# Values computed once a token and dealt to overlapping key blocks through DRAM, in a fused four-part kernel with a planned order

## The chip, the cores and the metric

One core of a Trainium2 chip runs the whole kernel. The engines named here are PE (matmuls; PEld is its weight load), DVE (vector), ACT (activations), POOL (general purpose) and SP, which only issues DMAs. The metric is device time in microseconds, the median of several runs; lower is better.

## The reference

Input `x` is (16, 256, 128) in fp32. Four parts follow each other, each normalised: a linear attention, a mixture of experts, a linear attention with feature maps, and then a stack of six layers of windowed attention and a gated feed-forward. Only this last stack, called the layer stage below, is touched by the change. One of its attention layers, with 16 heads of 64 and windows of 32 tokens:

```
qkv = x @ Wqkv
q, k, v = (sh(q), sh(k), sh(v))
q = l2norm(q) * qs
k = l2norm(k) * ksc
q = q * cos * scale + rotate_half(q) * sin * scale
k = k * cos * inv + rotate_half(k) * sin * inv
...
bk2, bv2 = (look(bk), look(bv))
mask = (it < jb) | (it > jb + w) | (jb == -1)
sim = jnp.einsum('bhwie,bhwje->bhwij', bq, bk2) * QK_SCALE
sim = jnp.where(mask, -jnp.finfo(sim.dtype).max, sim)
attn = jax.nn.softmax(sim, -1)
out = jnp.einsum('bhwij,bhwje->bhwie', attn, bv2)
...
return out @ Wo
```

`look` puts the window before in front of each window, so that a window of 32 queries sees 64 keys and each key and value is used by two windows. Each layer adds its result to x, then a layernorm, two products with an exact Gelu gate and a third product are added as well.

## The kernel before

Tokens lie in tiles of 128 (four windows). A sequence has two tiles (`TPS`), a unit two sequences (`SPU`), and there are eight units; the layer stage therefore does 6 x 32 = 192 tiles. x stays in SBUF, transposed (`xs`, features on the partitions), with 32 columns of zeros ahead of each sequence for the window before the first.

The stages before the layers are written in order. The layer stage is not: every piece of work is a `step` with an engine, an estimated duration in us, the steps that it follows, the buffers that it takes and uses, and a rank (the running number of its tile, lower first). `Plan.run` plays this through once at build time, with its own estimates, a lag after each step (`LAG`) and a price for changing the activation table (`SWITCH`), and issues each step when its turn comes. The result is a fixed order of instructions on each engine; on the chip every engine goes through its own list in that order and waits where an operand is missing. Buffers are counted: PSUM is four `pair`s of two banks (a `bank` is half of one).

A tile in `projections` (lines 738 to 834): `product` makes q, then k, in a pair each (L748); ACT squares them (L801); DVE multiplies with the cosine and sine tables (L755, L762) and sums the squares (L771); POOL adds the two products (L810). `norms` calls `inv_norm`, eleven small DVE operations on 128x32 values (L726 to L735), three Newton rounds from a guess by bits. POOL scales q and k by it (L777), PE transposes them (L783) and ACT copies them into `qT` and `kT` (L789).

A tile in `attention` (lines 836 to 977): `scores` is 64 small matmuls, 64x32 by 64 columns (L851). In fp32 a matmul is issued as two instructions, with a weight load for each, so this is 128 matmul records and 128 weight loads. DVE adds the mask in PSUM (`mask`, L860), takes the maximum (`top`, L864) and subtracts it on the way to SBUF (`below`, L869); ACT takes exp (L878); PE transposes (L899), ACT copies (L956). `values` computes v anew for every key block: each of the four blocks of 64 tokens is the stationary operand, twice, for the even and the odd heads (L885), and ACT copies the result to `va` (L892). `mix` multiplies the exponentials with `va`, which has a column of ones so that the sum comes with it (L911); DVE divides (L922, L923), PE transposes, ACT copies to `oT` (L929).

`output` runs once a sequence: 8 matmuls over 256 columns (L985), then DVE adds to x (L994). `feed_forward` runs once a unit; its Gelu needs another activation table than exp, and is preceded by a table load. `Seq.gate` lets the projections of a tile start only when `below` of the tile three before (`AHEAD`) is done. The weights of a layer are loaded by `fetch_a` and `fetch_f` on SP into one of two sets of buffers, for the layer after the next use.

Of the kernel before, what the change touches and what calls it, by code (L numbers as in the profile page):

```python
# [10 lines left out]
F32 = mybir.dt.float32  # L11
# [6 lines left out]
P = 128  # L18
# [15 lines left out]
AHEAD = 3  # L34
NEXP = 8
# [14 lines left out]
class Step:  # L50


    def __init__(self, eng, work, fn, after, takes, uses, rank, table):
        self.eng, self.work, self.fn, self.rank = eng, work, fn, rank
        self.takes, self.uses, self.table = takes, uses, table
        self.next, self.wait = [], 0
        for b in (*takes, *uses):
            b.left += 1
        for s in after:
            s.next.append(self)  # L60
            self.wait += 1


class Plan:
# [3 lines left out]
    LAG = 0.12  # L68
    SWITCH = 1.3

# [4 lines left out]
    def step(self, eng, work, fn, after=(), takes=(), uses=(), rank=0, table=None):  # L75
        s = Step(eng, work, fn, [a for a in after if a is not None], takes, uses, rank, table)
        self.steps.append(s)
        return s
# [30 lines left out]
    def run(self):  # L109
# [11 lines left out]
        now, table, opened = 0.0, None, {}  # L121
        left = len(self.steps)
        self.log = []
        while left:
            moved = True
            while moved:
                moved = False
                for eng, heap in ready.items():
# [3 lines left out]
                    while heap and len(back) < 64:  # L132
                        item = heapq.heappop(heap)
                        s = item[2]
                        if s.table and opened and s.table not in opened:
                            back.append(item)
                            continue
                        kinds = [b.kind for b in s.takes]
                        if all(self._fits(kinds, k) for k in set(kinds)):
                            got = s  # L140
                            break
                        back.append(item)
# [27 lines left out]
                    heapq.heappush(events, (now + work + self.LAG, count, got))  # L170
# [16 lines left out]
        self.end = now  # L187

# [18 lines left out]
def tile_kernel(ctx: ExitStack, tc: tile.TileContext, a: dict, out: bass.AP):  # L207
# [64 lines left out]
    def load_attn_weights(wp, i):  # L272
        w = {}
        w["qkv"] = load(wp, [P, 3 * INNER], a["L1_ffn_Wqkv"][i], "d_wqkv")
        w["o"] = load(
            wp, [P, 8, P], a["L1_ffn_Wo"][i].rearrange("(c p) d -> p c d", p=P), "d_wo"
        )
        w["sc"] = load_bc(wp, 4 * DH, a["qk_scale"][i], "d_sc")
        return w

    def load_ffn_weights(wp, i):
# [395 lines left out]
    with ExitStack() as st:  # L677
# [3 lines left out]
        sd = st.enter_context(tc.tile_pool(name="sd", bufs=4))  # L681
# [6 lines left out]
        for b in range(NB):  # L688
# [9 lines left out]
            "va": several(cd, 2, [P, NB, 8, DH + 1], "d_va"),  # L698
# [6 lines left out]
            "oT": several(cd, 2, [P, 8, SEQ], "d_oT"),  # L705
# [6 lines left out]
        for va in slots["va"]:  # L712
            pool.memset(va[:, :, :, DH : DH + 1], 1.0)
# [9 lines left out]

        def inv_norm(x, n):

            dve.tensor_scalar(x, x, 1e-24, None, ALU.max)  # L726
            y = sd.tile([P, n], F32, name="d_ny")
            t = sd.tile([P, n], F32, name="d_nt")
            dve.tensor_scalar(
                y.bitcast(I32), x.bitcast(I32), -0.5, 1597463007.0, ALU.mult, ALU.add  # L730
            )
            for _ in range(3):
                dve.tensor_tensor(t, y, y, ALU.mult)
                dve.scalar_tensor_tensor(t, t, -0.5, x, ALU.mult, ALU.mult)
                dve.scalar_tensor_tensor(y, t, 1.5, y, ALU.add, ALU.mult)  # L735
            return y

        def projections(q, t):
# [34 lines left out]
            def norms():  # L773
                o.rn = inv_norm(o.ss.rearrange("p g h -> p (g h)"), 2 * HEADS)
# [18 lines left out]
            for qk in range(2):  # L793
                pj, sq, t1, t2 = Buf("pair"), Buf("sq"), Buf("t1"), Buf("t2")
                mm = step(
                    "pe", 1.72, partial(product, qk, pj), [*q.ready, *q.loaded, q.gate(t)],
                    [pj], rank=rank,
                )
                s = step(
# [5 lines left out]
                a2 = step("dve", 1.14, partial(second, qk, pj, t2), [mm, q.tabbed], [t2], [pj], rank)  # L805
                reds.append(step("dve", 1.14, partial(squares, qk, sq), [s, *reds], [], [sq], rank))
# [8 lines left out]
            nm = step("dve", 2.5, norms, reds, rank=rank)  # L815
# [4 lines left out]
            for qk in range(2):  # L820
# [3 lines left out]
                tn = step("pe", 0.88, partial(turn, t1s[qk], pz), [m], [pz], [t1s[qk]], rank)  # L824
# [11 lines left out]
        def attention(q, t):  # L836
# [4 lines left out]
            pS, e, va, eT, y = Buf("pair"), Buf("e"), Buf("va"), Buf("eT"), Buf("y")  # L841

            def scores():

                for c in range(8):
# [12 lines left out]
            def mask():  # L858
                s3 = pS.t.rearrange("p (h k) -> p h k", k=2 * WIN)
                dve.tensor_tensor(s3, s3, bc(win[:, t, :], [P, HEADS, 2 * WIN], 1), ALU.add)  # L860

            def top():
                o.m = sd.tile([P, HEADS], F32, name="d_m")
                dve.tensor_reduce(  # L864
                    o.m, pS.t.rearrange("p (h k) -> p h k", k=2 * WIN), AX.X, ALU.max
                )

            def below():
                dve.tensor_tensor(  # L869
                    e.t.rearrange("p c a k -> p a c k"),  # L870
                    pS.t.rearrange("p (a c k) -> p a c k", a=2, k=2 * WIN),
                    bc(o.m.rearrange("p (a c) -> p a c", a=2), [P, 2, 8, 2 * WIN], 3),
                    ALU.subtract,
                )
# [5 lines left out]
            def values(b2, pv):  # L880
                wv = q.w["qkv"][:, 2 * INNER :].rearrange("p (c a d) -> p a c d", a=2, d=DH)
                for j in range(2):
                    x0 = t * P + (2 * b2 + j) * WIN
                    for par in range(2):
                        pe.matmul(  # L885
                            pv.t[par * DH : (par + 1) * DH, j * 512 : (j + 1) * 512],
                            lhsT=q.x[:, x0 : x0 + 2 * WIN], rhs=wv[:, par, :, :],
                            start=True, stop=True,
                        )

            def put_values(b2, pv):
                act.copy(  # L892
                    va.t[:, 2 * b2 : 2 * b2 + 2, :, 0:DH],
                    pv.t.rearrange("p (j c d) -> p j c d", j=2, d=DH),
                )

# [7 lines left out]
            def mix(hh, po):  # L904
                for k in range(4):
                    c = 4 * hh + k
                    for par in range(2):
                        r = slice(par * DH, (par + 1) * DH)
                        s0 = par * 512 + k * (DH + 1)
                        for b in range(NB):  # L910
# [3 lines left out]
                                rhs=va.t[r, b, c, :], start=True, stop=True,  # L914
# [13 lines left out]
            def put_out(pz):  # L928
                act.copy(  # L929
                    q.oT.t[:, :, t * P : (t + 1) * P],  # L930
                    pz.t.rearrange("p (c n) -> p c n", n=P),
                )

            sc = step("pe", 1.9, scores, [o.done[0], *q.turned[: t + 1]], [pS], [qT, kT], rank)
            mk = step("dve", 1.15, mask, [sc], [], [pS], rank)
            tp = step("dve", 1.15, top, [mk], [], [pS], rank)
            be = step("dve", 1.15, below, [tp], [e], [pS], rank)
            ex = step("act", 0.98, exps, [be], [], [e], rank, ("exp", 0))
            q.soft.append(be)
            vs = []  # L940
            for b2 in range(NB // 2):
                pv = Buf("pair")
                v = step(
                    "pe", 1.94, partial(values, b2, pv), [*q.ready, *q.loaded, mk], [pv], [], rank
                )
                vs.append(
                    step(
                        "act", 0.97, partial(put_values, b2, pv), [v],
                        [] if b2 else [va], [pv] + ([va] if b2 else []), rank,
                    )  # L950
                )
            pz = Buf("pair")
            te = step("pe", 0.88, partial(turn, e, pz), [ex], [pz], [e], rank)
# [5 lines left out]
            for hh in range(2):  # L959
                po = Buf("pair")  # L960
                mx = step("pe", 0.75, partial(mix, hh, po), [pe_, *vs], [po], [eT, va], rank)
                ds.append(
                    step(
                        "dve", 0.85, partial(divide, hh, po), [mx],
# [4 lines left out]
            ty = step("pe", 0.88, partial(turn, y, py), ds, [py], [y], rank)  # L969
            if t == 0:  # L970
                q.oT = Buf("oT")
            q.outs.append(
                step(
                    "act", 0.97, partial(put_out, py), [ty],
                    [] if t else [q.oT], [py] + ([q.oT] if t else []), rank,
                )
            )

        def output(q):

            pr = Buf("bank")

            def product():
                for c in range(8):
                    pe.matmul(  # L985
                        pr.t[:, :SEQ], lhsT=q.w["o"][:, c, :], rhs=q.oT.t[:, c, :],
                        start=(c == 0), stop=(c == 7),
                    )

            def add():  # L990
                for h2 in range(2):
                    hp = slice(h2 * DH, (h2 + 1) * DH)
                    xo = q.x[hp, WIN + h2 : WIN + h2 + SEQ]
                    dve.tensor_tensor(xo, pr.t[hp, :SEQ], xo, ALU.add)  # L994

            rank = q.rank + 1
# [269 lines left out]
```

## Time and profile before

Three runs took 5848.07, 5855.04 and 5859.02 us. The profiled execution took 5849.97 us.

| | |
|---|---|
| span of the profiled execution | 5848.2 us |
| instructions | 153345 |
| granted PE clock, mean | 0.942 of full speed |
| DMA packets, volume | 29195, 40.16 MB |
| first projection (L748) to last feed-forward sum (L1073) | 1647.3 to about 5814 us |

The profile shows one execution. Busy times are unions of an engine's instructions of a group; "idle before" is the time in which the engine stood just before instructions of a group, with what ended that wait. PE's instructions overlap each other, so a group's busy time over its number is the better price of one than the mean duration. A wait for several things is put down to the one that came last. The rows of digits cut the span into 40 equal slices of 146 us, each digit being tenths.

The mean of one and the number, for the groups in the layer stage that the diff touches and that are not shown below:

| group | number | mean us |
|---|---|---|
| scores L851, PE (busy 309.2 us in all) | 24576 | 0.232 |
| mix L911, PE (busy 301.1 us in all) | 24576 | 0.228 |
| mask L860, DVE | 192 | 1.228 |
| top L864, DVE | 192 | 1.220 |
| below L869, DVE | 192 | 1.218 |
| norm, L733, L734, L735, DVE | 576 each | 0.192 |
| output sum L994, DVE | 192 | 0.423 |
| exp L878, ACT | 192 | 1.059 |
| copy to oT L929, ACT | 192 | 1.010 |

### The profile page before, as it was taken

Reading aid. Unit: us, or ns where it says so; the run is one execution under the profiler, and the core shown is the slowest. Engines: PE = TensorE matmul, PEld = TensorE weight load, DVE = VectorE, ACT = ScalarE, POOL = GpSimd, SP = SyncE. Lnnn points to the kernel's source line nnn. Section 1 sums busy time; section 2 is a strip of 40 time slices with the busy share of each in tenths; the row PEclk is TensorE's granted clock in tenths of the full one; section 3 lists DMA queues with packets and bytes.
Section 4 is the critical chain, followed back from the end, with each engine's and each line's share of the span. In section 5 each row is a group of like instructions: output and inputs, shape, how many; then the busy total and the mean of one; then the engine's idle time right before and its main releaser. Section 6 shows DMA issues by size and latency. Waiting matters only on the chain. (4 is left out here: it accounts for less than half of the span.)

```text
span 5848.2 us, 153345 instructions
## 1 busy us (share of the span) xinstructions
PE 4866.8 (83%) x69216; PEld 3086.3 (53%) x69216; DVE 4182.3 (72%) x7764; ACT 2325.8 (40%) x2701; POOL 1951.1 (33%) x964
## 2 busy tenths in 40 slices
PE   4677778787788888888888888898898888888886
PEld 3444566566655555555555555555555555555554
DVE  3333777777777777777678777777777777777775
ACT  1343112111134444444444444444444444444443
POOL 0000222222234344344344334334334434434432
PEclk7898899999999999999999999999999999999998
DMA  1000000000000000000000000000000000000001
GB/s 37 13 1 20 1 2 2 4 3 2 2 25 2 2 2 13 10 2 2 2 17 6 2 2 2 21 2 2 2 2 21 2 2 2 2 2 2 2 2 30
DMA packets 29195, 40.16 MB, mean 7 GB/s; under 512 B 5118, under 2 KB 24060, under 8 KB 27772
## 3 DMA queue, kind: packets, MB, share of 16 engines
q1 hardware_dynamic: 28540, 30.35, 1.7%
q8 instruction: 543, 8.90, 0.6%
q14 instruction: 112, 0.92, 0.1%
HBM read 26.15 MB, written 4.19 MB: 5 GB/s over the span
## 5 line engine op out<-in xcount | busy, mean ns | idle before, releaser
L810 POOL TENSOR_TENSOR d_t<-d_t,d_t 128x1024 f32<-128x1024 f32 x384 | 905.3, 2363 | 1717.1 <-DVE d_t L762 1242.4
L777 POOL TENSOR_TENSOR d_t<-d_t,d_ny 128x1024 f32<-128x1024 f32 x384 | 722.7, 1903 | 520.4 <-DVE d_ny L735 515.9
L748 PE MATMUL pp<-d_wqkv,xs 128*128 128x512 f32 x1536 | 776.4, 636 | 85.0 <-ACT d_oT L929 49.6
L885 PE MATMUL pp<-d_wqkv,xs 128*64 128x512 f32 x3072 | 753.5, 624 | 76.2 <-DVE d_t L762 75.2
L755 DVE TENSOR_TENSOR d_t<-pp,d_tab 128x1024 f32<-128x1024 f32 x384 | 467.8, 1218 | 392.7 <-PE pp L748 392.6
L801 ACT ACTIVATE d_sq<-pp 128x1024 f32<-128x1024 f32 x384 | 388.6, 1025 | 756.2 <-PE pp L748 250.6
L892 ACT COPY d_va<-pp 128x1024 f32<-128x1024 f32 x384 | 383.5, 1011 | 530.5 <-PE pp L885 529.5
L783 PE MATMUL pp<-ident,d_t 128*128 128x128 f32 x3072 | 414.0, 282 | 119.5 <-ACT d_qT L789 85.3
L762 DVE TENSOR_TENSOR d_t<-pp,d_tab 128x1024 f32<-128x1024 f32 x384 | 467.1, 1216 | 50.3 <-ACT d_sq L801 50.3
L783 PEld LDWEIGHTS pp<-ident,d_t 128*128 128x128 f32 x3072 | 354.3, 145 | 246.3 <-issue 158.9
L569 POOL TENSOR_TENSOR c_e<-c_e,c_sm 128x2048 f32<-128x2048 f32 x64 | 231.7, 3621 | 757.0 <-DVE c_sm L568 682.1
L748 PEld LDWEIGHTS pp<-d_wqkv,xs 128*128 128x128 f32 x1536 | 279.4, 200 | 375.5 <-issue 228.9
L771 DVE TENSOR_REDUCE d_ss<-d_sq 128x16 f32<-128x1024 f32 x384 | 464.9, 1211 | 1.4
L885 PEld LDWEIGHTS pp<-d_wqkv,xs 128*64 128x64 f32 x3072 | 202.2, 142 | 489.1 <-issue 344.1
L851 PE MATMUL pp<-d_kT,d_qT 64*32 64x64 f32 x24576 | 309.2, 232 | 157.2 <-issue 103.8
L851 PEld LDWEIGHTS pp<-d_kT,d_qT 64*32 64x32 f32 x24576 | 266.1, 108 | 225.0 <-issue 158.9
L911 PE MATMUL pp<-d_va,d_eT 64*32 64x65 f32 x24576 | 301.1, 228 | 85.5 <-issue 41.5
L985 PE MATMUL pp<-d_oT,d_wo 128*128 128x256 f32 x1536 | 357.1, 385 | 1.8 <-ACT d_oT L929 1.3
L911 PEld LDWEIGHTS pp<-d_va,d_eT 64*32 64x32 f32 x24576 | 261.1, 106 | 180.6 <-issue 90.7
L564 ACT ACTIVATE c_e<-c_e 128x2048 f32<-128x2048 f32 x64 | 122.4, 1912 | 566.2 <-DVE c_e L562 552.3
L985 PEld LDWEIGHTS pp<-d_oT,d_wo 128*128 128x128 f32 x1536 | 284.0, 190 | 113.0 <-ACT f_h L1051 38.5
L929 ACT COPY d_oT<-pp 128x1024 f32<-128x1024 f32 x192 | 193.9, 1010 | 331.7 <-PE pp L899 252.3
(172 smaller groups left out, 8440.2 us busy)
## 6 DMA issues: line engine op xcount, KB each, us to landing
d_wqkv<-L_ffn_Wqkv SPq DMA_DIRECT2D x6, 1536.0 KB, 7.1
d_wo<-L_ffn_Wo SPq DMA_DIRECT2D x6, 512.0 KB, 4.0
xin<-L_attn_x SPq DMA_DIRECT2D x8, 256.0 KB, 2.9
keep<-xu SPq DMA_DIRECT2D x8, 256.0 KB, 2.0
d_y<-keep SPq DMA_DIRECT2D x8, 256.0 KB, 2.7
out<-d_y SPq DMA_DIRECT2D x8, 256.0 KB, 2.3
d_w<-L_ffn_W SPq DMA_DIRECT2D x6, 341.0 KB, 3.0
b_w<-b_w SPq DMA_DIRECT2D x3, 576.0 KB, 7.4
```

The costliest lines, as they stand in the source:

```text
L748: pe.matmul(pj.t[:, hf * 512 : (hf + 1) * 512], lhsT=xj, rhs=q.w["qkv"][:, c : c + 512], start=True, stop=True,)
L755: dve.tensor_tensor(t1.t, heads(pj.t), bc(q.lay.tab[:, 0, t, cc], hs, 1), ALU.mult)
L762: dve.tensor_tensor(t2.t.rearrange("p h (x d) -> p h x d", x=2), swapped(pj.t), bc(q.lay.tab[:, 1, t, cc].rearrange("p (x d) -> p x d", x= ...
L771: dve.tensor_reduce(o.ss[:, qk, :], sq.t, AX.X, ALU.add)
L777: pool.tensor_tensor(t1.t, t1.t, bc(o.rn[:, qk * HEADS : (qk + 1) * HEADS], hs, 2), ALU.mult)
L783: pe.transpose(pz.t[:, c * P : (c + 1) * P], t1.t[:, 2 * c : 2 * c + 2, :].rearrange("p h d -> p (h d)"), ident,)
L801: lambda sq=sq, pj=pj: act.activation(sq.t, heads(pj.t), AF.Square),
L810: lambda t1=t1, t2=t2: pool.tensor_tensor(t1.t, t1.t, t2.t, ALU.add),
L851: pe.matmul(pS.t[b * WIN : (b + 1) * WIN, s0 : s0 + 2 * WIN], lhsT=qT.t[r, c, b * WIN : (b + 1) * WIN], rhs=kT.t[r, c, k0 : k0 + 2 * WIN], ...
L885: pe.matmul(pv.t[par * DH : (par + 1) * DH, j * 512 : (j + 1) * 512], lhsT=q.x[:, x0 : x0 + 2 * WIN], rhs=wv[:, par, :, :], start=True, st ...
L911: pe.matmul(po.t[b * WIN : (b + 1) * WIN, s0 : s0 + DH + 1], lhsT=eT.t[r, c, b * WIN : (b + 1) * WIN], rhs=va.t[r, b, c, :], start=True, s ...
L985: pe.matmul(pr.t[:, :SEQ], lhsT=q.w["o"][:, c, :], rhs=q.oT.t[:, c, :], start=(c == 0), stop=(c == 7),)
```

## The change

The planner gets a lag for each engine instead of one for all, 2 us for a DMA, and a rule: a step of more than 32 PE instructions is put off while, with it, more than 256 PE instructions would be issued within 3.6 us. `scores` is cut into four steps and `mix` into two for each half.

The mask is added on the way from PSUM to `e` in SBUF, `top` reads `e`, and `below` runs on POOL, in place. The norm's guess comes from ACT, as exp(-0.5 ln x), with one Newton round on DVE.

`values` multiplies a tile of 128 tokens once with the weights of v. ACT copies the result to `vs`, which has the columns of ones; SP writes it to a DRAM buffer `dv` of the sequence (`away`), 32 rows of zeros standing ahead of it, and reads it back into `va` (`windows`) with the overlapping rows, for the even heads to the lower 64 partitions and for the odd heads to the upper ones. The output product and its addition to x run for each tile; the addition waits for all steps of the sequence that read x. q, k, v weights keep two places and the other weights of a layer have one, loaded after their last use in the layer before.

```diff
-    LAG = 0.12
+    LAG = {"pe": 0.25, "act": 0.15, "dve": 0.12, "pool": 0.15, "sp": 2.0}
     SWITCH = 1.3
+
+    BLOCK, SPAN = 256, 3.6
...
+                        if s.count > 32 and self._dense(s, now, past, events):
+                            back.append(item)
+                            continue
...
+    def _dense(self, s, now, past, events):
+
+        room = self.BLOCK - s.count
+        for t, c in reversed(past):
+            room -= c
+            if room < 0:
+                wait = t + self.SPAN - s.work
+                if wait > now + 1e-6:
+                    self.unique -= 1
+                    heapq.heappush(events, (wait, self.unique, None))
+                    return True
+                return False
+        return False
...
-            "va": several(cd, 2, [P, NB, 8, DH + 1], "d_va"),
+            "va": several(cd, 3, [P, NB, VR], "d_va"),
+            "vs": several(cd, 2, [P, 2, VR], "d_vs"),
+            "dv": several(dr, 2, [WIN + SEQ, 2, VR], "d_dv"),
...
-            "oT": several(cd, 2, [P, 8, SEQ], "d_oT"),
+            "oT": several(cd, 3, [P, 8, P], "d_oT"),
...
-            def norms():
-                o.rn = inv_norm(o.ss.rearrange("p g h -> p (g h)"), 2 * HEADS)
+            def floor():
+                o.ss = o.ss.rearrange("p g h -> p (g h)")
+                dve.tensor_scalar(o.ss, o.ss, 1e-24, None, ALU.max)
+
+            def guess():
+                o.rn = sd.tile([P, 2 * HEADS], F32, name="d_rn")
+                act.activation(o.rn, o.ss, AF.Ln)
+                act.activation(o.rn, o.rn, AF.Exp, scale=-0.5)
+
+            def refine():
+                r = sd.tile([P, 2 * HEADS], F32, name="d_rt")
+                dve.tensor_tensor(r, o.rn, o.rn, ALU.mult)
+                dve.scalar_tensor_tensor(r, r, -0.5, o.ss, ALU.mult, ALU.mult)
+                dve.scalar_tensor_tensor(o.rn, r, 1.5, o.rn, ALU.add, ALU.mult)
...
-            nm = step("dve", 2.5, norms, reds, rank=rank)
+            fl = step("dve", 0.22, floor, reds, rank=rank)
+            gu = step("act", 0.45, guess, [fl], rank=rank, table=("exp", 0))
+            nm = step("dve", 0.68, refine, [gu], rank=rank)
...
             def mask():
-                s3 = pS.t.rearrange("p (h k) -> p h k", k=2 * WIN)
-                dve.tensor_tensor(s3, s3, bc(win[:, t, :], [P, HEADS, 2 * WIN], 1), ALU.add)
+                dve.tensor_tensor(
+                    e.t.rearrange("p c a k -> p a c k"),
+                    pS.t.rearrange("p (a c k) -> p a c k", a=2, k=2 * WIN),
+                    win[:, t, :].unsqueeze(1).unsqueeze(1).to_broadcast([P, 2, 8, 2 * WIN]),
+                    ALU.add,
+                )
...
             def below():
...
+                e3 = e.t.rearrange("p c a k -> p (c a) k")
+                pool.tensor_tensor(e3, e3, bc(o.m, [P, HEADS, 2 * WIN], 2), ALU.subtract)
...
+            def values():
+                xj = q.x[:, WIN + t * P : WIN + (t + 1) * P]
+                for hf in range(2):
+                    c = 2 * INNER + hf * 512
+                    pe.matmul(
+                        pv.t[:, hf * 512 : (hf + 1) * 512], lhsT=xj,
+                        rhs=q.w["qkv"][:, c : c + 512], start=True, stop=True,
+                    )
+
+            def put_values():
                 act.copy(
-                    va.t[:, 2 * b2 : 2 * b2 + 2, :, 0:DH],
-                    pv.t.rearrange("p (j c d) -> p j c d", j=2, d=DH),
-                )
+                    vs.t.rearrange("p a (c d) -> p c a d", d=DH + 1)[:, :, :, 0:DH],
+                    pv.t.rearrange("p (c a d) -> p c a d", a=2, d=DH),
+                )
+
+            def away():
+                sp.dma_start(out=q.dv.t[WIN + t * P : WIN + (t + 1) * P], in_=vs.t)
+
+            def windows():
+
+                row = 2 * VR
+                for par in range(2):
+                    src = q.dv.t[t * P : t * P + 2 * WIN, par, :]
+                    sp.dma_start(
+                        out=va.t[par * 2 * WIN : (par + 1) * 2 * WIN],
+                        in_=bass.AP(
+                            tensor=src.tensor, offset=src.offset,
+                            ap=[[row, 2 * WIN], [WIN * row, NB], [1, VR]],
+                        ),
+                    )
...
+            for g in range(4):
+                sc.append(
+                    step(
+                        "pe", 0.48, partial(scores, g), [o.done[0], *q.turned[: t + 1], *sc[-1:]],
+                        [] if g else [pS], [qT, kT] + ([pS] if g else []), rank, count=64,
+                    )
+                )
+            mk = step("dve", 1.15, mask, sc, [e], [pS], rank)
+            tp = step("dve", 1.14, top, [mk], [], [e], rank)
+            be = step("pool", 1.95, below, [tp], [], [e], rank)
...
+            vm = step("pe", 1.76, values, [*q.ready, *q.loaded, sc[-1]], [pv], [], rank, count=8)
+            ve = step("act", 0.97, put_values, [vm], [vs], [pv], rank)
+            vw = step(
+                "sp", 0.1, away, [ve], [] if t else [q.dv], [vs] + ([q.dv] if t else []), rank
+            )
+            q.dealt.append(vw)
+            vd = step("sp", 0.2, windows, q.dealt, [va], [q.dv], rank)
...
+                            "pe", 0.38, partial(mix, hh, g, po), [pe_, vd, *mx], [] if g else [po],
+                            [eT, va] + ([po] if g else []), rank, count=64,
...
+            mo = step("pe", 1.8, product, [os_, *q.loaded_o], [pr], [oT], rank, count=32)
+            q.sums.append((add, mo, pr, rank))
...
+            ls = step("sp", 0.3, fetch_sc, last.get(("t", i - 1), []), rank=base)
+            la = step("sp", 6.0, fetch_qkv, last.get(("qkv", i - 2), []), rank=base)
+            lo = step("sp", 3.0, fetch_o, last.get(("o", i - 1), []), rank=base)
+            lf = step("sp", 3.0, fetch_f, last.get(("f", i - 1), []), rank=base)
...
+                    for add, mo, pr, rank in q.sums:
+                        adds.append(step("dve", 0.6, add, [mo, *q.read], [], [pr], rank))
```

## The prediction

> **What bounds the kernel now.** I read the page's rows of busy time first, then the same engines over the six layers alone, then what PE waited for there, then the groups of instructions.
>
> ```profile
> PE 4866.8 (83%) x69216; PEld 3086.3 (53%) x69216; DVE 4182.3 (72%) x7764; ACT 2325.8 (40%) x2701; POOL 1951.1 (33%) x964
> PE   4677778787788888888888888898898888888886
> DVE  3333777777777777777678777777777777777775
> PEclk7898899999999999999999999999999999999998
> ```
>
> From the twelfth slice on, nothing changes any more: that is the layer stage, the only part that the change touches. It runs from the first projection (1647.3 us) to the last feed-forward sum (5814 us). The answer for this stretch, with length, then busy time of PE, weight load, DVE, ACT, POOL, then the granted clock:
>
> ```profile
> 1647.30:5814.00 4166.70, 3626.28 (x62696) 2193.10 (x62696) 3127.83 (x5676) 1929.15 (x2021) 1672.81 (x816) 0.96 0.02 6
> ```
>
> 4166.7 us for 6 x 16 x 2 = 192 tiles are 21.70 us a tile. PE is busy 18.89 of them (87%), DVE 16.29 (75%), ACT 10.05, POOL 8.71. So PE bounds the stage, with 540 us idle. Its largest waits there (us in total, times, longest):
>
> ```profile
> PE pp L851 <- issue: 103.8, 61, 2.6
> PE pp L783 <- ACT d_qT L789: 85.3, 46, 2.1
> PE pp L885 <- DVE d_t L762: 75.2, 59, 2.4
> PE pp L851 <- ACT d_kT L789: 51.8, 47, 1.1
> PE pp L748 <- ACT d_oT L929: 49.6, 45, 1.1
> PE pp L911 <- issue: 41.5, 37, 2.5
> ```
>
> Two kinds: "issue", where no operand is missing (151 us with its small rows), and evacuations that come late (230 us by ACT, 133 by DVE). The first kind in the order of time, at a scores burst followed by a mix:
>
> ```profile
> 3026.35 1.15 PEld L911 LDWEIGHTS pp<-d_va,d_eT 64*32 64x32 f32 x106
> 3026.36 1.29 PE L911 MATMUL pp<-d_va,d_eT 64*32 64x65 f32 x104
> 3029.89 0.66 PE L911 MATMUL pp<-d_va,d_eT 64*32 64x65 f32 x23 [2.24 <-issue]
> 3030.48 3.78 PE L748 MATMUL pp<-d_wqkv,xs 128*128 128x512 f32 x4
> ```
>
> After some 230 small instructions PE stands 2.24 us although nothing holds it; the following projection takes 3.78 us for what is 1.88 elsewhere. Scores and mix are 256 PE instructions each (128 matmuls and their weight loads), run in 1.5 us, so I read this as the instruction stream arriving too slowly.
>
> **The parts.** The groups that I price with (busy, mean ns):
>
> ```profile
> L777 POOL TENSOR_TENSOR d_t<-d_t,d_ny 128x1024 f32<-128x1024 f32 x384 | 722.7, 1903 | 520.4 <-DVE d_ny L735 515.9
> L748 PE MATMUL pp<-d_wqkv,xs 128*128 128x512 f32 x1536 | 776.4, 636 | 85.0 <-ACT d_oT L929 49.6
> L885 PE MATMUL pp<-d_wqkv,xs 128*64 128x512 f32 x3072 | 753.5, 624 | 76.2 <-DVE d_t L762 75.2
> L892 ACT COPY d_va<-pp 128x1024 f32<-128x1024 f32 x384 | 383.5, 1011 | 530.5 <-PE pp L885 529.5
> L985 PE MATMUL pp<-d_oT,d_wo 128*128 128x256 f32 x1536 | 357.1, 385 | 1.8 <-ACT d_oT L929 1.3
> L1051 ACT ACT_TABLE_LOAD x48 | 61.6, 1283 | 0.9
> ```
>
> *Values once a token.* Today 16 instructions a tile cost 753.5 us over the stage; afterwards four of the projection's own shape, half of the 1536 at L748, so 388 us. PE: **-365 us**, as PE is the bound. One of the two copies at L892 goes (-192 us of ACT, not on the path).
>
> *Output product per tile.* 32 instructions of 128 columns replace 16 of 256 in a sequence. Stage C has this very shape (L639): 512 instructions, 65.2 us, 0.127 us each, so 3072 x 0.127 = 391 against 357. **+34 us**. Its evacuation is only cut differently. The addition to x becomes 384 x 2 halves of 128 columns instead of 192 of 256; by the 0.29 us of the 128-column addition at L643 that is 384 x 0.29 = 111 against 81 us of DVE, +30. It waits now for every reader of x in its sequence; PE has issued them long before.
>
> *Scores in four steps, mixes in two, with a limit of 256 PE instructions in 3.6 us.* The work is the same; what can go is the issue wait, 0 to -151 us. A tile has about 650 PE instructions, 9.1 us at that rate, in some 20 us, so there is room. I take two thirds, **-100**.
>
> *DVE gets lighter.* `below` leaves (192 x 1.218 = 234 us); of the norm's eleven small operations four stay, so L729 (some 35 us) and two thirds of 3 x 110.6 go, 256 us. With the +30 DVE falls from 3128 to about 2670 us, 64%. The scores' pair of banks comes free after the mask, two DVE operations earlier than now. Of the 133 us in which PE waits for DVE I take **-50** (0 to -133). The new lags in the planner (0.25 us behind PE, where 0.12 stood) may also remove ACT waits; I count nothing for them.
>
> *`below` on POOL.* Its row is L777, also with a broadcast operand: 1.903 us, +365 us on POOL, 2038 in all, half of the stage. It queues there behind the two scalings (3.77 us in a row) and the two additions (2.36 each), with exp behind it, and the projections three tiles on wait for it. In between stands a margin of two tiles: **+20** (0 to +130, the 0.69 us excess each time).
>
> *Ln and Exp in the norm.* Two activations of 128x32; the nearest row, the sigmoid at L433 with this shape, took 0.198 us. The planner counts 0.45 for both, with no switch of tables.[...] If the sets are chosen function by function, each tile pays two loads: by the row 1.283 each, 2.57 us a tile, 493 us on ACT.[...] I give two loads 85%. ACT then goes to 1929 - 192 + 493 + 77 = 2307 us, 55%: not the bound. But behind the loads in ACT's queue stand squares, exponentials and evacuations, one for every 2 us of PE work; and the refinement, the two POOL scalings and the transposes of q and k come 2.5 us later than planned. ACT idles almost half the time, so it has caught up after some 5 us, with two evacuations late, which I price at 1 us of PE a tile: **+190** (0 if the joint set is chosen or the delay is hidden; +493 if all stands on PE).
>
> *The way through DRAM.* 128 rows of 4160 bytes out (532 KB), then two transfers of 532 KB each back. Neighbours (KB each, us to landing):
>
> ```profile
> d_wqkv<-L_ffn_Wqkv SPq DMA_DIRECT2D x6, 1536.0 KB, 7.1
> d_wo<-L_ffn_Wo SPq DMA_DIRECT2D x6, 512.0 KB, 4.0
> ```
>
> and 341 KB in 3.0. So 3.3 us out and 5.3 back (1065 KB, between the 4.0 and the 7.1), with three issues of about 0.35: 9.6 us, where the planner counts 0.1 + 2 + 0.2 + 2 = 4.3. From the scores' end: values 1.9, copy 1.0, way 9.6, so 12.5 us. Beside it runs the softmax, which in one undisturbed tile of the trace took 10.7 us from the end of the scores (4022.1) to the mix (4032.84), and which gets longer by the POOL queue and ACT's loads. The two ends nearly tie; mix is first in rank, so the planner sets it where it believes the rows have landed, and PE then waits with everything behind it. I take half a microsecond a tile, **+90** (0 to 192 x 5.1 = +980).
>
> *Instructions and data on the same engines.* 543 instruction packets carry 8.9 MB; 307 MB now join them, some 5 to 9 us of every tile. A fetch that meets them comes late: **+20** (0 to +150).
>
> *Weights and set-up.* The output and feed-forward weights have one place instead of two, so each layer loads them after the last use in the layer before. The first new use lies a tile (about 20 us) or more behind, the landing takes 4.0: hidden; uncovered 5 x 4 = 20. The scales and zeroed rows at the start: **+5**.
>
> Sum: -365 + 34 - 100 - 50 + 20 + 190 + 90 + 20 + 5 = **-156 us**, so 5850 (the profiled execution: span 5848.2 and 1.8 around it) becomes 5694. The median of the runs is 5855, 0.1% above it; I say **5695**.
>
> **Rivals.**
>
> *All is hidden* (15%): the joint set, or ACT's slack absorbs the loads; DMAs inside the softmax's time. -365 + 34 - 120 - 70 + 60 + 10 = -451, **5400**. For it: PE and DVE, the two fullest engines, both lose over 9%. Against: the order on each engine is fixed by a plan that is wrong by microseconds on two links.
>
> *The way through DRAM ends last* (26%), slower: at the first mix of each tile PE waits for the windows. Without the DMA's term the sum is -246 us, so from 1.3 us a tile on it decides. At half of the 5.1, 2.55 us x 192 = 490: 5850 - 246 + 490 = **6095**. For it: the planned 4.3 us against rows that give over 9. Against: other tiles' PE work can already lie between, and the softmax is as long.
>
> *The table loads stand wholly on PE* (14%): 493 instead of 190, **5998**.
>
> The forecast's own case, 5500 to 5838, has 40%; 5% are left for no change, within 0.2%, which is about what this measurement can tell. So faster 55%, same 5%, slower 40%. The range, 5430 to 6090, leaves out the lower half of the first rival and the upper half of the second.[...]
>
> **What will show it.** Values at half of the projection's busy time; no rows of PE waiting for "issue" at scores and mix; ACT_TABLE_LOAD near 430 in the layers (two a tile and those around Gelu), or about 95 if the joint set serves; PE's waits at mix named by the DMA, at transposes and projections by ACT; DVE near 2670 us; landings of 3 to 6 us. I am wrong if the windows take much more than 5.3 us, if the loads cost PE nothing or everything, or if the limit on instructions leaves PE standing for want of other steps.

## The result, and the profile after

The changed kernel takes 6158 us (6146 to 6162, four runs) where the kernel before takes 5852: a ratio of 1.052, 95% interval 1.050 to 1.053. It was forecast to be faster. The profiled execution took 6159.61 us, with a span of 6157.8.

The page's row of busy time, then the layer stage alone (1650.7 us, the first projection, to 6124.4, the last feed-forward sum; length, busy time of PE, weight load, DVE, ACT, POOL, granted clock, share of the DMA engines, GB/s):

```profile
PE 4811.9 (78%) x68448; PEld 3222.4 (52%) x68448; DVE 3878.6 (63%) x6420; ACT 2703.8 (44%) x3256; POOL 2313.6 (38%) x1157
```

```profile
1650.70:6124.40 4473.70, 3568.45 (x61928) 2326.60 (x61928) 2824.66 (x4334) 2309.03 (x2578) 2036.19 (x1013) 0.90 0.30 74
```

The stage grew from 4167 to 4474 us, by 307; that is the whole difference but for 3 us of set-up. Two things are to be seen. PE is idle for 905 us instead of 540. And PE is busy for 3568 us, only 58 less than before, although 365 us of matmuls left; the granted clock (the share of full speed at which PE was let run) fell from 0.96 to 0.90. What PE waited for in the layers (us in total, times, longest):

```profile
PE pp L958 <- DMA d_va<-d_dv: 393.6, 226, 5.9
PE pp L807 <- POOL d_t L801: 53.5, 30, 6.6
PE pp L946 <- ACT d_e L911: 51.4, 25, 4.6
PE pp L958 <- ACT d_eT L1017: 39.1, 25, 2.3
```

L958 is the mix: it waits for the windows of values, 2.05 us a tile. By kind, all rows of this view come to 394 us for the DMA (0 before), 220 for ACT (234), 220 for DVE (142), 54 for POOL (12) and 12 for issue (151). The transfers (KB each, median us to landing) and the table loads:

```profile
d_va<-d_dv SPq DMA_DIRECT2D x384, 520.0 KB, 6.7
d_dv<-d_vs SPq DMA_DIRECT2D x192, 520.0 KB, 3.2
```

```profile
L791 ACT ACT_TABLE_LOAD x192 | 246.3, 1283 | 3.4
L792 ACT ACT_TABLE_LOAD x192 | 246.3, 1283 | 3.4
```

One tile in the order of time, from its values to its mix (start us, us, engine, line):

```profile
3004.62 1.88 PE L917 MATMUL pp<-d_wqkv,xs 128*128 128x512 f32 x4
...
3006.36 1.28 ACT L792 ACT_TABLE_LOAD   x1
...
3007.79 1.00 ACT L923 COPY d_vs<-pp 128x1024 f32<-128x1024 f32 x1
...
3008.82 0.33 SPq L929 DMA_DIRECT2D d_dv<-d_vs  x1
...
3011.56 1.24 SPq L936 DMA_DIRECT2D d_va<-d_dv  x2
...
3014.42 1.01 ACT L1017 COPY d_eT<-pp 128x1024 f32<-128x1024 f32 x1
...
3016.80 0.32 PE L958 MATMUL pp<-d_va,d_eT 64*32 64x65 f32 x8 [2.08 <-DMA d_va<-d_dv]
...
3019.10 2.00 PE L958 MATMUL pp<-d_va,d_eT 64*32 64x65 f32 x120 [1.98 <-DMA d_va<-d_dv]
...
3021.02 3.71 PE L1088 MATMUL pp<-f_xn,d_w 128*85 128x512 f32 x4
```

The write goes out at 3008.82, the windows are issued when it has landed, the even heads' windows are there at 3016.8 and the odd heads' at 3019.1: 10.3 us, where the planner counted 4.3. The exponentials, the other operand, are in SBUF at 3015.43, so the DMA is 3.7 us late. The copy of the values itself had to wait 1.3 us, behind the table load. What follows adds to the wait: the feed-forward product at 3021.02 takes 3.71 us for what took 1.88 in the kernel before (3064.36). The same time in two stretches (length, PE busy, then the clock, the share of the DMA engines and GB/s):

```profile
3014.77:3018.18 3.41, 0.32 (x8) 1.00 0.99 193
3018.18:3025.01 6.83, 5.91 (x127) 0.50 0.01 4
```

PE stood for some 4 us, with eight small instructions in between, and then worked at half the clock for about 6.

### The profile page after: what moved, and what is told of

The parts are those of the page before. It is cut to its first block, busy times and chain, and to the rows that moved or that the text cites. A ratio compares the mean times of both kernels' runs of the same rounds, so it can differ in the third digit from the quotient of the medians.

```text
span 6157.8 us, 152108 instructions
## 1 busy us (share of the span) xinstructions
PE 4811.9 (78%) x68448; PEld 3222.4 (52%) x68448; DVE 3878.6 (63%) x6420; ACT 2703.8 (44%) x3256; POOL 2313.6 (38%) x1157
## 5 line engine op out<-in xcount | busy, mean ns | idle before, releaser
L837 POOL TENSOR_TENSOR d_t<-d_t,d_t 128x1024 f32<-128x1024 f32 x384 | 904.9, 2358 | 1299.9 <-DVE d_t L773 1184.5
L801 POOL TENSOR_TENSOR d_t<-d_t,d_rn 128x1024 f32<-128x1024 f32 x384 | 723.7, 1902 | 562.0 <-DVE d_rn L798 553.6
L759 PE MATMUL pp<-d_wqkv,xs 128*128 128x512 f32 x1536 | 794.3, 645 | 35.7 <-DVE d_t L773 23.3
L958 PE MATMUL pp<-d_va,d_eT 64*32 64x65 f32 x24576 | 419.0, 257 | 464.4 <-DMA d_va<-d_dv 393.6
L958 PEld LDWEIGHTS pp<-d_va,d_eT 64*32 64x32 f32 x24576 | 315.0, 120 | 698.6 <-issue 264.0
L766 DVE TENSOR_TENSOR d_t<-pp,d_tab 128x1024 f32<-128x1024 f32 x384 | 468.6, 1220 | 259.7 <-PE pp L759 188.1
L907 POOL TENSOR_TENSOR d_e<-d_e,d_m 128x1024 f32<-128x1024 f32 x192 | 365.4, 1903 | 501.5 <-DVE d_m L901 398.9
L917 PE MATMUL pp<-d_wqkv,xs 128*128 128x512 f32 x768 | 419.9, 674 | 23.8 <-DVE d_y L970 10.8
L980 PEld LDWEIGHTS pp<-d_oT,d_wo 128*128 128x128 f32 x3072 | 375.0, 196 | 113.4 <-ACT d_oT L976 60.4
L980 PE MATMUL pp<-d_oT,d_wo 128*128 128x128 f32 x3072 | 391.7, 282 | 46.6 <-ACT d_oT L976 35.3
L884 PE MATMUL pp<-d_kT,d_qT 64*32 64x64 f32 x24576 | 363.7, 230 | 48.4 <-ACT d_kT L813 36.5
L923 ACT COPY d_vs<-pp 128x1024 f32<-128x1024 f32 x192 | 195.7, 1019 | 390.5 <-PE pp L917 388.6
L813 ACT COPY d_qT<-pp 128x1024 f32<-128x1024 f32 x192 | 194.3, 1012 | 383.0 <-PE pp L807 379.8
```

Source lines behind the costliest of these rows:

```text
L759: pe.matmul(pj.t[:, hf * 512 : (hf + 1) * 512], lhsT=xj, rhs=q.w["qkv"][:, c : c + 512], start=True, stop=True,)
L766: dve.tensor_tensor(t1.t, heads(pj.t), bc(q.lay.tab[:, 0, t, cc], hs, 1), ALU.mult)
L801: pool.tensor_tensor(t1.t, t1.t, bc(o.rn[:, qk * HEADS : (qk + 1) * HEADS], hs, 2), ALU.mult)
L837: lambda t1=t1, t2=t2: pool.tensor_tensor(t1.t, t1.t, t2.t, ALU.add),
L884: pe.matmul(pS.t[b * WIN : (b + 1) * WIN, s0 : s0 + 2 * WIN], lhsT=qT.t[r, c, b * WIN : (b + 1) * WIN], rhs=kT.t[r, c, k0 : k0 + 2 * WIN], ...
L917: pe.matmul(pv.t[:, hf * 512 : (hf + 1) * 512], lhsT=xj, rhs=q.w["qkv"][:, c : c + 512], start=True, stop=True,)
```

## The experiments

Two theories were set against each other. **A**: the way of the values through DRAM ends last at each mix, and the stalls cost clock as well. **B**: the two table loads a tile delay the norm and ACT's evacuations, and the DMA waits are only where this shows.

| run | edit on the changed kernel | us | ratio to before, 95% interval | layer stage | PE busy, idle in it | clock in it |
|---|---|---|---|---|---|---|
| after | none | 6158 | 1.050 to 1.053 | 4474 | 3568, 905 | 0.90 |
| e1 | joint table set | 6073 | 1.037 to 1.041 | 4393 | 3561, 832 | 0.90 |
| e2 | values early | 5607 | 0.957 to 0.961 | 3925 | 3396, 529 | 0.95 |
| e3 | planner told the DMA's times | 5775 | 0.986 to 0.989 | 4089 | 3437, 652 | 0.95 |
| e4 | e1 and e2 | 5395 | 0.921 to 0.925 | 3710 | 3303, 407 | 0.97 |
| e5 | e1, values on PE as before | 5859 | 1.001 to 1.004 | 4174 | 3711, 462 | 0.98 |
| e6 | e4 and e3 | 5393 | 0.921 to 0.923 | 3707 | 3309, 398 | 0.97 |
| e7 | e4, no limit on PE instructions | 5569 | 0.951 to 0.954 | 3880 | 3371, 509 | 0.95 |
| e8 | e4, `below` on DVE | 5623 | 0.959 to 0.963 | 3918 | 3353, 565 | 0.97 |
| e9 | e2, planner told the guess's time | 5556 | 0.948 to 0.951 | 3870 | 3361, 509 | 0.97 |
| e10 | filling ahead of the mix | 6122 | 1.045 to 1.049 | 4451 | 3775, 676 | 0.95 |

**e1, the joint table set.**

```diff
+        def joint():
+            if tabset.get("set") != "joint":
+                act.preload_act_table_set("natural_log_exp_and_others")
+                tabset["set"] = "joint"
...
             def guess():
...
+                joint()
                 act.activation(o.rn, o.ss, AF.Ln)
...
+                joint()
                 act.activation(ef, ef, AF.Exp)
```

(The Gelu marks the set as gone.)

> Edit: the set of tables that holds both Ln and Exp is asked for by name, so that the two loads a tile (384 in all) go and only those after a Gelu stay; the planned order is the same. Theory A (the way of the values through DRAM ends last, and the stalls at mix also cost granted clock): PE still waits near 390 us at mix, the time falls by 30 to 120 us, to 6040-6130. Theory B (the loads delay the norm and ACT's evacuations, and the DMA waits are only where this delay shows): it falls by 250 us or more, below 5910.

The layers' loads fell to 48 before the Gelus and 48 after them, ACT's busy time there by 458 us, and the time by 86 us. PE waits for the DMA 449 us now, not less: what ACT no longer delays runs into the same late windows. This is A's answer; B wanted 250 us.

**e2, values early.** The step follows the k projection and no longer the scores.

```diff
-            vm = step("pe", 1.76, values, [*q.ready, *q.loaded, sc[-1]], [pv], [], rank, count=8)
+            vm = step("pe", 1.76, values, [*q.ready, *q.loaded, o.mm], [pv], [], rank, count=8)
```

> Edit: values no longer waits for the last scores of its tile but only for the k projection, so the write and the windows start some 10 us earlier; the tables stay. Theory A: the DMA wait at mix (394 us) goes to under 60 us, the granted clock rises from 0.90 to about 0.95, and the time falls by 350 to 600 us, to 5550-5810. Theory B: the time falls by less than 150 us, to above 6000, and the waits at mix are taken over by ACT and POOL.

The time fell by 552 us to 5607, below the kernel before. No DMA wait is left among PE's rows, though the landings are as long (6.8 us). The layer stage, columns as before:

```profile
1647.00:5572.10 3925.10, 3396.13 (x61932) 2203.96 (x61932) 2778.05 (x4333) 2283.75 (x2564) 2038.29 (x1013) 0.95 0.34 84
```

Of the 549 us that the stage lost, 376 were idle time of PE and 172 its busy time, with the same instructions at a clock of 0.95 instead of 0.90. A holds, in both of its halves.

**e3, the planner told the truth about the DMA.**

```diff
-    LAG = {"pe": 0.25, "act": 0.15, "dve": 0.12, "pool": 0.15, "sp": 2.0}
+    LAG = {"pe": 0.25, "act": 0.15, "dve": 0.12, "pool": 0.15, "sp": 2.9}
...
-                "sp", 0.1, away, [ve], [] if t else [q.dv], [vs] + ([q.dv] if t else []), rank
+                "sp", 0.33, away, [ve], [] if t else [q.dv], [vs] + ([q.dv] if t else []), rank
...
-            vd = step("sp", 0.2, windows, q.dealt, [va], [q.dv], rank)
+            vd = step("sp", 1.24, windows, q.dealt, [va], [q.dv], rank)
+            vd.more = 3.2
```

> Edit: only the planner's estimates for the two DMA steps are set to what was measured (issue 0.33 and 1.24 us, landing 3.2 and 6.7 us after issue); same work, another order. If the wait comes from the wrong estimate (theory A, mis-planned), the order hides most of it: PE's wait for the DMA under 150 us and 5800 to 6000 us. If the way is simply longer than the softmax beside it and nothing else can be put between, the wait becomes idle time by plan and the time stays within 60 us of 6158. Theory B: within 60 us as well, but with the DMA waits gone.

5775, somewhat better than the range given, with 16 us of DMA waits. The work, the buffers and the step that the transfers' chain starts from are those of the changed kernel; only the order differs. So 383 of e2's 552 us can be had by the order alone, with the way as long as it is.

**e4, both.**

> Edit: e1 and e2 together. Theory A with the tables as a smaller second term: 5450 to 5700, below the kernel before (5852), and lower than e2 by 50 to 150 us. Theory B: the gain over e1 is under 150 us. If the two overlap (both only shift the same waits), e4 is within 30 us of the better of the two.

5395, 7.7% below the kernel before, and below the range given. The layer stage, and PE's two largest waits in it:

```profile
1646.90:5357.10 3710.20, 3303.26 (x61932) 2155.15 (x61932) 2802.91 (x4333) 1844.77 (x2216) 2039.24 (x1013) 0.97 0.36 89
```

```profile
PE pp L814 <- POOL d_t L808: 41.9, 47, 4.2
PE pp L955 <- ACT d_e L920: 40.4, 29, 3.9
```

No single wait stands out any more, and PE is busy for 3303 us. The loads are worth 212 us here (e2 to e4), where 50 to 150 were expected, and 86 in e1, where the DMA ended last anyway.

**e5, the values on PE again.** The values for every key block and their two copies are taken from the kernel before; the DRAM buffer is gone, the rest is e1.

```diff
-            vm = step("pe", 1.76, values, [*q.ready, *q.loaded, sc[-1]], [pv], [], rank, count=8)
...
+                v = step(
+                    "pe", 1.94, partial(values, b2, pv), [*q.ready, *q.loaded, sc[-1]], [pv], [], rank, count=16
+                )
```

> Edit: e1 (joint set) with the values computed for every key block on PE as in the kernel before, without the DRAM buffer; all else of the change stays. It shows what the new way of the values is worth by itself: against e4 (5395), where that way is hidden, and e1 (6073), where it ends last. Theory A: PE's busy time in the layers rises by about 365 us over e4's 3303, the granted clock is 0.95 or more, and the time is 5650 to 5800: better than e1 by 270 to 420, worse than e4 by 250 to 400. Theory B: above 5950, since then the rest of the change is what costs.

5859: outside A's range by 59 us and below B's. Against e4 the new way of the values, together with its early start, is worth 464 us; against e1, where it is not hidden, it costs 214. And everything else in the change, even with the joint set, is worth nothing by itself: 5859 against 5848. It takes away 78 us of PE's idle time (issue waits 151 to 2), and adds 85 us of PE busy time: 33 in the output product (357 to 390), 51 in the scores (309 to 360) and 28 in the mix (301 to 329), although the mean of one is no longer (223 and 226 ns, before 232 and 228), so they overlap less with their neighbours; part of this is made up elsewhere. Whether values on PE would gain from an early start as well was not run.

**e6, e4 with the DMA's times told.** `e3`'s edit on e4.

> Edit: e4 with the planner told the measured DMA times. Theory A: with the early start nothing waits for the DMA, so within 50 us of 5395. If the planner's order still suffers from the wrong estimate: lower by more than 50.

5393: no difference, as A has it. The early start leaves the estimate without effect.

**e7, no limit on PE instructions.**

```diff
-    BLOCK, SPAN = 256, 3.6
+    BLOCK, SPAN = 1 << 20, 3.6
```

> Edit: e4 with the limit on PE instructions out of reach, so that scores and mix steps follow each other as their operands allow. If the limit is what takes the issue waits away (151 us before, 76 in e4): issue waits rise to 120-200 us and the time by 40 to 150, to 5435-5545. If the limit only spreads work that would not stall: within 30 us of 5395 or lower.

5569, 174 us more than e4: more than expected, while the issue waits rose less, from 76 to 113 us.

```profile
PE pp L892 <- issue: 71.7, 31, 5.7
...
PE pp L967 <- issue: 30.8, 20, 4.1
```

The rest is PE's other idle time (+66 us) and busy time (+67), with a clock of 0.95 against 0.97. The busy time is the clock: PE is busy at half clock for 366 us, in e4 for 167, and half of the difference is 100. Which part of the idle time follows from the stalls and which from another order of all the work was not separated.

**e8, the subtraction on DVE.**

```diff
-                pool.tensor_tensor(e3, e3, bc(o.m, [P, HEADS, 2 * WIN], 2), ALU.subtract)
+                dve.tensor_tensor(e3, e3, bc(o.m, [P, HEADS, 2 * WIN], 2), ALU.subtract)
...
-            be = step("pool", 1.95, below, [tp], [], [e], rank)
+            be = step("dve", 1.15, below, [tp], [], [e], rank)
```

> Edit: e4 with the subtraction of the maximum on DVE again, in place in SBUF. DVE's busy time rises by 234 us, POOL's falls by 365. By the prediction's term (20 us for the longer step on POOL) the time stays within 60 us of 5395; if POOL's queue holds the softmax up, it falls by more than 60; if DVE is the next bound, it rises by more than 60.

5623, 228 us slower. DVE goes from 2803 to 3116 us in the stage, 76% to 80% of it, and PE's waits for DVE from 168 to 236, for POOL from 44 to 88, although POOL has less to do: its scalings wait 599 us for the norm on DVE, where they waited 386. So the longer step on POOL paid. DVE's rise is 313 us where 234 were expected, for this is not the step of the kernel before, which read PSUM: between two places in SBUF the 104 subtractions that start while POOL is idle take 1.22 us on average, the 88 that start while POOL works 2.36.

**e9, the planner told what the guess takes.**

```diff
-            gu = step("act", 0.45, guess, [fl], rank=rank, table=("exp", 0))
+            gu = step("act", 3.0, guess, [fl], rank=rank, table=("exp", 0))
```

> Edit: e2 with the planner told that the norm's guess takes 3.0 us on ACT instead of 0.45; the two table loads a tile stay. If the loads' 212 us (e2 against e4) come from the order being planned without them: the time falls to within 70 us of e4, 5400 to 5470. If the loads cost by themselves, as ACT time in a long chain: within 50 us of e2's 5607.

5556, between the two: 51 us of the 212 come back by an honest estimate, 161 stay. Most of what the loads cost is not undone by planning with them; that it is their time in a chain that PE follows is the likely reading, not shown by itself.

**e10, filling ahead of the mix.**

```diff
             def mix(hh, g, po):
+                if hh == g == 0:
+                    for _ in range(2):
+                        pe.matmul(
+                            po.t[:, 0:512], lhsT=ident,
+                            rhs=rope.rearrange("p a t d -> p (a t d)"), start=True, stop=True,
+                        )
```

> Edit: the kernel after the change, with two matmuls of 128x512 (1.9 us of PE a tile, 361 us in all, written to the bank that the first mix then overwrites, from constants) just ahead of the first mix, unknown to the planner. They stand where PE waits for the DMA. If the stalls at mix also cost clock (PE busy is 265 us above e4's with the same instructions): the clock rises to 0.94 or more and the time stays at 6158 or falls, by up to 200 us, in spite of the added work. If only the waits count and the clock does not depend on them: the part of the filling that is not inside a wait comes on top, 6200 to 6450.

6122, 36 us faster with 386 us of matmuls more (busy time of their line, L954). The stage, and its first wait:

```profile
1651.30:6102.10 4450.80, 3774.93 (x62696) 2367.39 (x62696) 2822.01 (x4333) 2309.03 (x2578) 2036.29 (x1013) 0.95 0.30 74
```

```profile
PE pp L964 <- DMA d_va<-d_dv: 196.4, 137, 4.8
```

The waits fell by 197 us only, so the filling did not fit into them alone. But PE's busy time rose by 206 us only, with the clock at 0.95 instead of 0.90. So the loss of clock is real, and in this kernel came from PE standing still at the mix.

## Why the prediction was wrong

**The step that failed** is the way through DRAM. The prediction put it as "the two ends nearly tie ... I take half a microsecond a tile, +90". Taking that wait away (e2) is worth 552 us, six times as much: 376 of it idle time of PE, 172 clock. With this in place of the 90, its sum is 5694 - 90 + 552 = 6156, against 6158 measured, which is luck in part, since the other terms below are off as well and cancel. It was wrong in two ways:

- The length was nearly right, 9.6 us predicted and 10.3 in the tile shown (windows 7.5 instead of 5.3), but the write started late: the last scores end at 3002.80, the values are multiplied 1.8 us later and their copy waits another 1.3, so that the windows are complete 16.3 us after the scores, where the prediction had 12.5. The softmax took 12.6. The two ends do not tie. What was mis-sized above all is how much of the difference between 10 and the planner's 4.3 reaches PE. The mix stands in PE's order where the planner believed it ready, all that comes after it waits too, and that happens in every tile: 2.05 us of wait. e3 shows that other work was there to be put between.
- The sum had no term at all for clock. With the same instructions PE is busy 3568 us in the changed kernel and 3303 in e4: 265 us, of which 172 go with the DMA's waits (e2) and 93 with the table loads. The granted clock in the layer stage accounts for it: PE is busy at half clock for 715 us in the changed kernel (159 stretches), 354 in e2 (83) and 167 in e4 (42), and half of 715 - 167 is 274, an estimate of what half a clock cost (work of 1.88 us took 3.71 and 3.78 at 0.50). The profile before already showed it, in the projection of 3.78 us after a stall of 2.24, a line that the prediction quoted and read as instruction fetch alone:

```profile
3024.99:3028.40 3.41, 1.50 (x128) 1.00 0.03 7
3028.40:3035.23 6.83, 5.34 (x33) 0.50 0.01 2
```

In the changed kernel's layers the stretches at half clock lasted 3.41 us or a multiple of it. PE need not have been idle for the whole of the 3.41 us before such a fall: in the lines above it was busy for 1.50 us of them, and over the changed kernel's layers for a third at the median and up to 55%.

The rival "the way through DRAM ends last", given 26%, is what happened. Its 6095 lies within 63 us, though by other parts: it took 490 us of wait and none of clock, where the wait is 394 (2.05 us a tile for its 2.55). The 5.1 us that it halves should be 5.3 by the prediction's own figures, 9.6 less 4.3, which moves it by 19 us only.

**The other terms.**

- *Values*, -365: right. Busy time at that line is 389 us in e4, for 753 before. Freed of waits, and with the early start, they are worth 464 in all (e5 to e4).
- *Output product*, +34: right, 382 to 392 us against 357. The addition to x comes in 384 halves, not 384 x 2, and took 110 us of DVE where the prediction had 111.
- *Issue waits*, -100: they fell by 139, from 151 to 12; but the cut steps themselves cost busy time, which was not counted (e5). In e4 the limit is worth 174.
- *DVE*, -50: wrong in sign in the changed kernel, where PE's waits for DVE rose from 142 (133 in the prediction, which left the small rows out) to 220. DVE's load fell to 2825 us, 155 short of the fall in the sum; the norm's four operations (L787, L796 to L798) take 291 us, where the sum kept 186, because those at L787 and L796 show 635 and 422 ns on average. They stand behind POOL: the 62 at L787 that start while POOL is idle take at most 183 ns, the 130 others 855 on average, and all 90 above 400 ns end within 0.25 us of the end of POOL's instruction. Of the 130, 112 start under the additions on POOL (L837) and 9 under `below` (L907). No term allowed for this.
- *`below` on POOL*, +20: not seen by itself. With `below` on DVE e4 is 228 us slower (e8), which counts DVE's relief and POOL's longer step together; the prediction had -50 for all of DVE and +20.
- *Table loads*, two a tile, +190: two there are, 384 of 1.283 us. Worth 86 us while the DMA ends last and 212 once it does not, within the bounds of 0 and 493. The joint set, one that serves both ln and exp, did not come about by itself: it had to be asked for by name, and then no load was left but the 48 before and 48 after the Gelus (e1). The 77 us that the prediction adds to ACT for the two activations are about twice 0.198 us a tile; they took 0.229 us each, 88 in all.
- *Instruction fetch beside the data*, +20: what it cost PE is not settled, and no run shows the 20. In the trace of the changed kernel's layers, the 101 instruction packets of 16 KB that overlap more than 16 data packets took 1.26 us on average (up to 2.02), the 385 others 1.13. Issue waits are 12 us in the changed kernel and 76 in e4, which moves as much data in less time. In e5, under the same limit and without that data, they are 2 us, and in no run with it under 11; the orders differ too.

**What stays open**: why e7 costs 174 us with only 36 more of issue waits, and how far each order that the planner makes is good or bad by chance; no run measures that spread.

## What to carry to other kernels

When the order of work is fixed by a planner, look first at the steps whose estimates were never measured, DMA landings above all: here a link counted at 4.3 us took 10.3 and was paid with 2.05 us of PE's wait a tile, and telling the planner the truth recovered 383 us without any other change. A transfer that depends on little should start as early as its operands allow, not beside the step that it feeds (552 us in e2). Stalls of PE should be priced with the clock as well as with the wait: here 394 us of waits came with 172 us of lost clock.

## What the runs showed of the hardware

- In the changed kernel a DMA that reads 520 KB from DRAM into 64 partitions, in four runs of 2080 bytes each, two of them issued together, landed 6.7 us after issue (median; 5.0 to 8.9), and took 0.59 us to issue. A write of 520 KB from 128 partitions in runs of 4160 bytes took 3.2 (2.6 to 8.5), with 0.33 to issue.
- In the changed kernel's layers every stretch at half clock lasted 3.41 us or a multiple of it. Taken in windows of this length, PE was busy for at most 55% of each of the 159 windows before a fall to half clock, and for at least 42% of each of the 887 after which full clock stayed; it came back after windows with 81% or more. So 1.5 us of standing in one window was enough in one case, and more than 2.0 was enough in every case.
- Adding 386 us of matmuls where PE stood idle made the kernel 36 us faster (e10), with a granted clock of 0.95 in the stage instead of 0.90.
- A DVE operation of 128x32 between places in SBUF (L787 in the changed kernel) took 174 ns on average when it started with POOL idle and 855 when POOL was working; all 90 above 400 ns ended within 0.25 us of the end of POOL's instruction. The product of 128x1024 that reads PSUM (L766) took 1.22 us either way.
- With the way through DRAM the DMA engines were busy for 30 to 36% of the stage; beside that the ACT and POOL rows of unchanged shape kept their durations (square on ACT 1.025 before and 1.021 after, addition on POOL 2.363 and 2.358).
